# A graph network in one kernel: the ranks of its edge sort counted by partition, and uneven transfers cut in two

## The chip, the cores and the metric

The kernel runs on one core of one Trainium2 chip. A core has five engines that run side by side and wait for each other through semaphores: TensorE (PE) for matrix products, VectorE (DVE), ScalarE (ACT), GpSimd (POOL) and SyncE (SP), which here only issues transfers. Sixteen DMA engines move data between the chip's memory (DRAM) and the on-chip memory, SBUF, of 128 partitions. Products land in PSUM, from which DVE or ACT take them. The metric is the time of one execution on the device, in microseconds (us); lower is better.

## What is computed

Two graph layers on 6250 nodes of 128 features, with 100000 edges (source, destination, weight, 128 edge features), sorted by destination. Each ends in a layer norm over the residual.

```python
# layer 0: two graph convolutions
def gcn_conv(x, src, dst, ew, W, b):
    deg = segment_sum(ew, dst); dinv = where(deg > 0, rsqrt(deg), 0)
    norm = dinv[src] * ew * dinv[dst]
    return segment_sum((x @ W)[src] * norm[:, None], dst) + b
x = layernorm(x + sigmoid(gcn_conv(relu(gcn_conv(x, W1, b1)), W2, b2)))   # with self-loops
# layer 1: attention over edges
z = x @ fc_w.T;  rh = edge_attr @ fc_r_w.T
e = leaky_relu(z[src] @ aw0 + z[dst] @ aw1 + rh @ aw2)
alpha = softmax of e over the edges of one dst
x = layernorm(x + relu(segment_sum(alpha[:, None] * (z[src] + rh), dst) + z @ loop_w))
```

## The kernel before

The edges stand in 49 chunks of 2048 (`CC`), the last of 1696. In a chunk, partition p holds the 16 edges 16p to 16p + 15 (`TC` = 16). As edges are sorted by destination, the destinations of one chunk fall into a window of 144 nodes (`WC`).

Each of the three passes over the edges has to fetch one row of a node table for every edge. Most rows come from a copy of the table in SBUF (`hot`, 48 blocks of 128 nodes as three bf16 parts), picked by products with one-hot masks. For this, the edges of a chunk are once sorted by the source's block: each of the 48 blocks (`BP`) has 32 slots (`CAP`) per chunk. An edge whose rank in its block is 32 or more, or whose source lies in the last block, goes to one of five further groups of 128 slots, whose rows GpSimd fetches from DRAM one by one (`far`, an indirect transfer, L485). Each of these five groups may only reach a fixed part of the window (`far_parts`). If an edge falls outside, or a group overflows, a flag in `odd` starts a slow path at the end.

The sort (`sort`, from L689) runs in batches of up to seven chunks, and beside the first pass. Its generator is stepped by `sort_to` between the pieces of the pass: seven steps that work out the ranks, then seven that place the edges (`ohm`, `ohg`, `put`, the products rec), then one that writes the slots' sources to DRAM (`srd`), from which the pass loads them as a row copied to all partitions (L849) and makes the masks (L853).

A rank step before (L698 to L723): `oh` is the one-hot of each edge's block, 128 x (48 x 16). The rank of an edge is the number of edges of the same block that stand before it, by its place t in the partition and then by partition. That number is summed in PSUM in two halves of 24 blocks (tile r, one buffer of two banks): a product with the strict triangle `trib` counts those of the same t on lower partitions; products with ones count the earlier t, by sums over 2, 4 and 8 places that DVE makes (`a2`, `a4`, `a8`, L703 to L705; the profile calls all three a). ACT copies r to bf16 (`own`, L717), DVE multiplies with `oh` and adds up over the 48 blocks, which leaves one rank for each edge.

In the pass itself (the loop after L860) `pick` makes the products g (L476), ACT scales them (`got`, L481), DVE makes the one-hot of the destinations (`wm`, L491 and L498), ACT weighs the far part of it (L515), and `scatter` sums rows by destination (win, L522). DVE adds the window to the accumulator `acc` (L527). The order of instructions in this stage is the scheduler's; each engine then runs its own list in order.

The second pass has its order written out by hand. Beside it DVE works out the edge scores from the edge features: `load_chunk` loads the next chunk's features (`et`, 16 x 128 numbers on each partition, L994, two buffers), `edge_dots` multiplies and reduces (L980, L981). After the pass the score stage begins, whose first instructions on DVE are a memset of `zero` (L1035) and on SP's queue two stores of it (`adgd`), then loads of source rows (`rk`) and masks.

Where the number of rows is no multiple of 128, a transfer covers what is left: 106 rows of the last node block (L231, L265), 106 partitions of the last chunk (L994), 49 rows of `degr` (L827), and 34, 82 or 114 rows of the softmax (`ad`, L1106).

## Time and profile before

| | |
|---|---|
| time, median of 3 runs | 2352.22 us (2351.19 to 2368.92) |
| the profiled execution | 1995.56 us, of which the span is 1993.8 us |
| mean granted clock of TensorE in it | 0.897 |

The profiled execution is a single one, and shorter than those that were timed. By stages, each row being the busy time in us of PE, PE's weight loads, DVE, ACT and POOL, then the granted clock (1 is full speed), the busy share of the DMA engines, and GB/s:

```profile
0.00:100.00 100.00, 52.41 (x462) 38.92 (x463) 75.07 (x199) 16.95 (x27) 25.95 (x192) 0.98 0.20 50
...
400.00:450.00 50.00, 42.88 (x1105) 38.84 (x1106) 43.79 (x105) 27.51 (x95) 35.48 (x29) 0.97 0.45 130
...
650.00:700.00 50.00, 43.92 (x672) 38.92 (x665) 17.69 (x31) 30.52 (x98) 25.05 (x20) 0.84 0.27 60
...
900.00:1000.00 100.00, 87.81 (x2033) 82.22 (x2033) 93.88 (x106) 69.92 (x225) 83.54 (x55) 0.93 0.75 243
...
1200.00:1300.00 100.00, 50.23 (x873) 40.25 (x874) 73.50 (x199) 22.02 (x53) 16.18 (x12) 0.58 0.50 142
...
1600.00:1700.00 100.00, 87.28 (x1955) 80.73 (x1956) 92.41 (x212) 38.39 (x132) 37.43 (x32) 0.93 0.66 184
```

From 0 to 170 us: loads, degrees, the first table, the first chunks' ranks. To about 640: the first pass with the sort. To 730: the second table. To about 1205: the second pass with the edge scores' dot products. Then the attention stage. In the page's lines and in the timeline, "a<-b" is what an instruction writes and reads, "[3.46 <-ACT own L717]" the time that its engine stood before it and what released it; neighbours of one kind are merged, with their number behind x.

The instructions of a rank step, as groups over 170 to 610 us (busy us in all, mean ns of one, then idle time before them):

```profile
L718 DVE TENSOR_TENSOR own<-own,oh 128x768 bf16<-128x768 bf16 x39 | 21.6, 555 | 21.3 <-ACT own L717 20.9
L698 DVE TENSOR_TENSOR oh<-iota_t,blk 128x768 bf16<-128x768 bf16 x37 | 20.0, 549 | 0.0
...
L703 DVE TENSOR_TENSOR a<-oh 128x384 bf16<-128x384 bf16 x38 | 13.5, 354 | 0.1
L723 DVE TENSOR_REDUCE rank<-own 128x16 f32<-128x96 bf16 x39 | 12.4, 318 | 0.1
...
L704 DVE TENSOR_TENSOR a<-a 128x192 bf16<-128x192 bf16 x38 | 9.6, 254 | 0.6
...
L705 DVE TENSOR_TENSOR a<-a 128x48 bf16<-128x48 bf16 x38 | 7.6, 201 | 0.7
```

These are durations from fetch to end; neighbours on one engine overlap a little, so that the distance from start to start is shorter.

### The profile page before, as it was taken

The page shows a single profiled execution, that of the slowest core. Times are in us where ns is not written, and L with a number is a line of the kernel's source. Part 1 is how long each engine was busy: PE and PEld are TensorE (multiplying, and loading weights), DVE is VectorE, ACT ScalarE, POOL GpSimd, SP SyncE. Part 2 cuts the span into 40 slices and gives each one's busy share as a digit, 9 for nine tenths or more (in the row PEclk, how much of TensorE's full clock was granted, in tenths as well). Part 3 has the DMA queues.
Part 4 walks back from the last instruction along what each step waited for, and adds up shares of the span by engine and source line. Part 5 has one row for each costly group of instructions (what it writes and reads, how often), then busy time and mean ns, then how long its engine had stood idle before and what let it go on. Part 6 is the DMA issues. An engine that isn't in the chain of part 4 may idle for free.

```text
span 1993.8 us, 78720 instructions
## 1 busy us (share of the span) xinstructions
PE 1594.7 (80%) x33767; PEld 1441.7 (72%) x33767; DVE 1633.2 (82%) x3252; ACT 945.4 (47%) x3098; POOL 1105.1 (55%) x953
## 2 busy tenths in 40 slices
PE   2867889989988868789888873568888888988996
PEld 1556878878877757688778762457777778877985
DVE  7788978988976348999989965889989898997764
ACT  1255445455455655667667653123444343435543
POOL 4025666677776548888888861214344353535762
PEclk9978989999998859999989995579999998999998
DMA  2114244244246237777777773646666566655663
GB/s 63 37 44 151 66 117 132 51 139 135 68 123 183 70 123 224 223 237 251 233 226 248 229 235 116 173 106 170 181 162 191 168 183 181 181 163 143 189 171 70
DMA packets 254593, 306.90 MB, mean 154 GB/s; under 512 B 37857, under 2 KB 193255, under 8 KB 247182
## 3 DMA queue, kind: packets, MB, share of 16 engines
q1 hardware_dynamic: 222627, 244.90, 38.9%
q0 software_dynamic: 23520, 48.22, 11.6%
q10 hardware_dynamic: 8088, 8.65, 1.4%
q8 instruction: 268, 4.39, 0.9%
q14 instruction: 90, 0.74, 0.1%
HBM read 260.42 MB, written 41.25 MB: 151 GB/s over the span
## 4 chain that ended last, share of the span: by engine, by line
DVE 38%; PE 37%; DMA 10%; issue 7%; ACT 5%; DVEq 1%; POOL 1%; SPq 0%; ACTq 0%; POOLq 0%
PE win L522 17%; PE g L476 6%; DVE wm L491 6%; DVE et L980 3%; DVE sel L1096 2%; DVE put L764 2%; DVE ohm L759 2%; DMA et<-in_edge_attr_dram 2%; PE rec L1209 2%; PE k L1093 2%; PE mm L333 2%; DMA rk<-srow 2%; ACT got L481 2%; DMA far<-g,sidx 1%; PE r L1239 1%
## 5 line engine op out<-in xcount | busy, mean ns | idle before, releaser
L485 POOL DMA_INDIRECT far<-g,sidx x490 | 729.2, 1488 | 228.4 <-PE win L522 101.1
L481 ACT ACTIVATE got<-g,swt 128x128 f32<-128x128 f32 x1764 | 484.9, 382 | 367.1 <-PE g L476 167.1
L485 POOL DMA_INDIRECT far<-zd,sidx x245 | 310.9, 1269 | 462.4 <-PE win L522 339.5
L522 PE MATMUL win<-wm,got 128*128 128x144 f32 x3528 | 529.1, 308 | 11.6 <-issue 11.5
L522 PEld LDWEIGHTS win<-wm,got 128*128 128x128 f32 x3528 | 492.1, 206 | 29.6 <-issue 20.2
L476 PE MATMUL g<-hot,mask 128*32 128x128 bf16 x21168 | 385.5, 226 | 81.3 <-issue 58.0
L476 PEld LDWEIGHTS <-mask 128*32 128x32 bf16 x21168 | 328.3, 100 | 117.3 <-issue 85.6
L491 DVE TENSOR_TENSOR wm<-iota,sdst 128x1728 f32<-128x1728 f32 x147 | 286.7, 1950 | 3.6 <-DMA g<-rows 3.5
L515 ACT ACTIVATE wm<-wm,swt 128x64 f32<-128x64 f32 (+1 forms) x735 | 201.2, 356 | 83.0 <-DVE wm L498 50.7
L522 PE MATMUL win<-wm,far 128*128 128x64 f32 (+1 forms) x1470 | 189.7, 274 | 19.7 <-DMA far<-g,sidx 15.5
L522 PEld LDWEIGHTS win<-wm,far 128*128 128x128 f32 x1470 | 184.8, 196 | 19.5 <-issue 15.8
L980 DVE TENSOR_TENSOR et<-et,ar_row 128x2048 f32<-128x2048 f32 (+1 forms) x49 | 111.6, 2278 | 25.2 <-DMA et<-in_edge_attr_dram 25.2
L527 DVE TENSOR_TENSOR acc<-acc,win 128x144 f32 x147 | 44.3, 301 | 106.1 <-PE win L522 93.4
L1093 PE MATMUL k<-adp,rk 128*128 128x49 bf16 x2352 | 92.1, 194 | 47.6 <-DVE sel L1096 33.2
L1093 PEld LDWEIGHTS <-rk 128*128 128x128 bf16 x2352 | 84.4, 103 | 59.3 <-issue 30.0
L981 DVE TENSOR_REDUCE dots<-et 128x16 f32<-128x2048 f32 (+1 forms) x49 | 112.0, 2286 | 1.7
L322 POOL TENSOR_TENSOR hot<-low,hot 128x512 bf16<-128x512 f32 x24 | 32.6, 1358 | 140.1 <-DVE hot L321 100.3
L1096 DVE TENSOR_TENSOR sel<-k,ohb 128x392 f32<-128x392 f32 x98 | 83.7, 854 | 4.5 <-PE k L1093 3.9
L764 DVE TENSOR_TENSOR put<-ohg,rec 128x1360 bf16<-128x1360 bf16 x49 | 76.8, 1566 | 0.0
L717 ACT CAST own<-r 128x768 bf16<-128x768 f32 x49 | 39.3, 802 | 70.9 <-PE r L714 50.0
L771 PE MATMUL rec<-put,ohm 128*128 128x90 bf16 x784 | 59.3, 242 | 15.6 <-DVE put L767 14.7
L771 PEld LDWEIGHTS <-ohm 128*128 128x128 bf16 x784 | 55.2, 164 | 21.6 <-DVE put L767 10.8
(397 smaller groups left out, 2317.7 us busy)
## 6 DMA issues: line engine op xcount, KB each, us to landing
et<-in_edge_attr_dram SPq DMA_DIRECT2D x97, 512.0 KB
et<-in_edge_attr_dram SPq DMA_DIRECT2D x48, 1024.0 KB
mask<-masks SPq DMA_DIRECT2D x98, 384.0 KB
rk<-srow SPq DMA_DIRECT2D x98, 256.0 KB
mask<-srd SPq DMA_DIRECT2D x49, 384.0 KB
masks<-mask SPq DMA_DIRECT2D x49, 384.0 KB
far<-g,sidx POOLq DMA_INDIRECT x490
g<-rows SPq DMA_DIRECT2D x24, 256.0 KB
```

Of the source, the lines that this page charges most:

```text
L476: nc.tensor.matmul(ps[32 * q : 32 * q + 32, g, :], mask[:, (g0 + g) * P + 32 * q : (g0 + g) * P + 32 * q + 32], hot[:, 4 * (g0 + g) + q, k ...
L481: nc.scalar.activation(got[:, g, :], ps[:, g, :], AF.Copy, scale=swt[:, c, g0 + g : g0 + g + 1])
L485: nc.gpsimd.indirect_dma_start(out=got, out_offset=None, in_=table[:, :], in_offset=bass.IndirectOffsetOnAxis(ap=sidx[:, c, g : g + 1], ax ...
L491: nc.vector.tensor_tensor(wm[:, : GP * WC].rearrange("p (g w) -> p g w", w=WC), iota[:, None, 1 : WC + 1].to_broadcast([P, GP, WC]), sdst[ ...
L515: nc.scalar.activation(m, m, AF.Copy, scale=swt[:, c, g : g + 1])
L522: nc.tensor.matmul(ps[:, n0 : n0 + m.shape[-1]], rows[g], m, start=g == 0, stop=g == G - 1)
L764: nc.vector.tensor_tensor(put[:, :, : G * F].rearrange("p t (g f) -> p t g f", f=F), ohg[:, :, :, None].to_broadcast([P, TC, G, F]), rec[: ...
L771: nc.tensor.matmul(ps, ohm[:, :, t], put[:, t, :], start=t == 0, stop=t == TC - 1)
L980: nc.vector.tensor_mul(et[:n], et[:n], ar_row[:n, None, :].to_broadcast([n, TC, D]))
L981: nc.vector.tensor_reduce(dots[:n, c, :], et[:n], AX.X, OP.add)
L1093: nc.tensor.matmul(ps[:, s, :], mk[:, s * P : (s + 1) * P], adp[:, 0, k, :NB], start=k == 0, stop=k == 2)
L1096: nc.vector.tensor_mul(sel, ps, ohb.rearrange("p b s -> p s b"))
```

## The change

The rank is counted in another order: by partition first, the partitions taken in a scattered order (partition p at place 79p mod 128), and within a partition by t. `first` is the 128 x 128 table of which partition comes before which, and `lower` the 16 x 16 table of which t comes before which. All edges of earlier partitions are counted by 16 products, one for each t, of `first` with the 48 columns `oh[:, :, t]`, summed in one PSUM tile of 128 x 48 with two buffers. The columns of such a product stand 16 elements (32 bytes) apart. ACT spreads the 48 counts to 48 x 16 as it copies them. Within the partition, DVE compares the 16 blocks with each other (`pairs`), multiplies by `lower` and reduces to 16 numbers (`near`); `near` is added to the ranks once for each batch. The sums a2, a4, a8 and the old products are gone.

Apart from that, a helper `even` cuts a number of rows into the largest multiple of 16 and the rest, and the uneven transfers are issued as two: 106 as 96 and 10, 49 as 48 and 1, 34, 82 and 114 as 32, 80 and 112 and 2.

```diff
@@ constants
+    spread = const.tile([P, P + 1], I32, name="spread")
+    for of, at in ((iota_i[:, :P], slice(0, P)), (iotap_i[:, 0:1], slice(P, P + 1))):
+        nc.vector.tensor_scalar(spread[:, at], of, 79, None, op0=OP.mult)
+        nc.vector.tensor_scalar(spread[:, at], spread[:, at], P - 1, None, op0=OP.bitwise_and)
+    spread_f = const.tile([P, P + 1], F32, name="spread_f")
+    nc.vector.tensor_copy(spread_f, spread)
+    first = const.tile([P, P], BF16, name="first")
+    nc.vector.tensor_scalar(first, spread_f[:, :P], spread_f[:, P:], None, op0=OP.is_gt)
+    lower = const.tile([P, TC, TC], BF16, name="lower")
+    nc.vector.tensor_tensor(lower, iotab[:, None, :TC].to_broadcast([P, TC, TC]),
+                            iotab[:, :TC, None].to_broadcast([P, TC, TC]), op=OP.is_lt)
@@ helper
+    def even(n):
+        cut = n // 16 * 16
+        return [slice(a, b) for a, b in ((0, cut), (cut, n)) if b > a]
@@ store_blocks (load_some, degr, load_chunk, softmax's ad in the same way)
-            eng.dma_start(table[(NB - 1) * P : N, :], of[:tail, NB - 1 - b0, :])
+            for r in even(tail):
+                eng.dma_start(table[(NB - 1) * P + r.start : (NB - 1) * P + r.stop, :], of[r, NB - 1 - b0, :])
@@ load_chunk
-                nc.sync.dma_start(ets[c][:n], ea[c * CC : c * CC + n * TC, :].rearrange("(p t) f -> p t f", t=TC))
+                of = ea[c * CC : c * CC + n * TC, :].rearrange("(p t) f -> p t f", t=TC)
+                for r in even(n):
+                    nc.sync.dma_start(ets[c][r], of[r])
@@ sort
-    ps_r = sorting.enter_context(tc.tile_pool(name="ps_r", bufs=1, space=PSUM))
+    ps_r = sorting.enter_context(tc.tile_pool(name="ps_r", bufs=2, space=PSUM))
...
+            near = sp.tile([P, BATCH, TC], F32, name="near", bufs=1)
...
-                a2 = sp.tile([P, BP, 8], BF16, name="a2")
-                a4 = sp.tile([P, BP, 4], BF16, name="a4")
-                a8 = sp.tile([P, BP, 1], BF16, name="a8")
-                nc.vector.tensor_tensor(a2, oh[:, :, 0:8], oh[:, :, 8:16], op=OP.add)
-                nc.vector.tensor_tensor(a4, a2[:, :, 0:4], a2[:, :, 4:8], op=OP.add)
-                nc.vector.tensor_tensor(a8, a4[:, :, 0:1], a4[:, :, 2:3], op=OP.add)
-                ps = ps_r.tile([P, 2, 512], F32, name="r")
-                for h in range(2):
-                    ks = slice(h * HB, h * HB + HB)
-                    full = ps[:, h, : HB * TC].rearrange("p (k t) -> p k t", t=TC)
-                    nc.tensor.matmul(full, trib, oh[:, ks, :], start=True, stop=False)
-                    nc.tensor.matmul(full[:, :, 8:16], onesb, oh[:, ks, 0:8], start=False, stop=False)
-                    for of, m, w in ((a2, 2, 4), (a4, 4, 2), (a8, 8, 1)):
-                        to = full.rearrange("p k (b i) -> p k b i", b=m)[:, :, :, w : 2 * w]
-                        nc.tensor.matmul(to, onesb, of[:, ks, None, 0:w].to_broadcast([P, HB, m, w]),
-                                         start=False, stop=w == 1)
+                ps = ps_r.tile([P, BP], F32, name="r")
+                for t in range(TC):
+                    nc.tensor.matmul(ps, first, oh[:, :, t], start=t == 0, stop=t == TC - 1)
+                pairs = sp.tile([P, TC, TC], BF16, name="pairs", bufs=1)
+                nc.vector.tensor_tensor(pairs, blk[:, c, :, None].to_broadcast([P, TC, TC]),
+                                        blk[:, c, None, :].to_broadcast([P, TC, TC]), op=OP.is_equal)
+                nc.vector.tensor_mul(pairs, pairs, lower)
+                nc.vector.tensor_reduce(near[:, c - c0, :], pairs, AX.X, OP.add)
                 own = sp.tile([P, BP, TC], BF16, name="own", bufs=2)
-                nc.scalar.copy(own.rearrange("p (h k) t -> p h (k t)", h=2), ps[:, :, : HB * TC])
+                nc.scalar.copy(own, ps[:, :, None].to_broadcast([P, BP, TC]))
                 nc.vector.tensor_mul(own, own, oh)
...
+            nc.vector.tensor_add(r_, r_, near[:, :n])
```

More of the change, by code (lines that the diff above doesn't have):

```diff
@@ L76, in gnn_kernel @@
     BP = 4 * GP
-    HB = BP // 2
     G = GP + GS
@@ L264, in load_some @@
         if b0 + n >= NB:
-            eng.dma_start(to[:tail, NB - 1 - b0, :], of[(NB - 1) * P : N, :])
+            for r in even(tail):
+                eng.dma_start(to[r, NB - 1 - b0, :], of[(NB - 1) * P + r.start : (NB - 1) * P + r.stop, :])
     def transpose_blocks(pool, to, of, first=0, count=NB):
@@ L826, in gnn_kernel @@
             degr = xp.tile([NB, 3, P], F32, name="degr")
-            nc.sync.dma_start(degr, degd.rearrange("k b p -> b k p"))
+            for r in even(NB):
+                nc.sync.dma_start(degr[r], degd.rearrange("k b p -> b k p")[r])
             nc.vector.tensor_add(degr[:, 0, :], degr[:, 0, :], degr[:, 1, :])
@@ L1105, in softmax @@
             ad = lp.tile([P, P], F32, name="ad", bufs=1)
-            nc.sync.dma_start(ad[:R, :], adgd[c0 * CC : c0 * CC + R * P].rearrange("(r j) -> r j", j=P))
+            rows = adgd[c0 * CC : c0 * CC + R * P].rearrange("(r j) -> r j", j=P)
+            for r in even(R):
+                nc.sync.dma_start(ad[r, :], rows[r, :])
             ps = ps_c.tile([P, P], F32, name="rec")
```

## The prediction

> **What bounds the kernel now.** I read the page first, then the busy times of the stage that the change touches (170 to 610 us, the first edge pass, in which the sort runs beside the aggregation), then its chain of waits, its waits, and last the timeline at two places.
>
> ```profile
> span 1993.8 us, 78720 instructions
> PE 1594.7 (80%) x33767; PEld 1441.7 (72%) x33767; DVE 1633.2 (82%) x3252; ACT 945.4 (47%) x3098; POOL 1105.1 (55%) x953
> ```
> ```profile
> 170.00:610.00 440.00, 384.36 (x8477) 352.62 (x8475) 381.23 (x815) 225.86 (x784) 307.49 (x209) 0.93 0.38 109
> ```
> The second fence is one row of the busy times by stretch: PE, PEld, DVE, ACT, POOL, then the granted clock. PE and DVE are each busy 87% of the stage. Neither has room: what one engine gives up is worth something only where the other does not wait already.
>
> ```profile
> by line: PE win L522 17.5%; DVE wm L491 9.8%; DVE put L764 9.5%; DVE ohm L759 8.3%; PE g L476 7.7%; issue 4.6%; DMA mask<-srd 4.5%; PE r L714 4.0%; PE rec L771 3.1%; ACT own L717 2.9%; ACT got L481 2.6%; DVE ohg L761 2.5%; PE r L710 2.4%; D
> ```
> ```profile
> PE rec L738 <- DVE tot L736: 22.8, 6, 5.9
> ...
> DVE own L718 <- ACT own L717: 20.9, 13, 2.9
> ...
> PE r L710 <- ACT own L717: 13.9, 6, 3.5
> ```
> First the chain of waits of that stretch, then its waits (us, times, longest). Adding up the chain's pieces, the rank products r (L710, L711, L714) hold 31.5 us of these 440, the sums a2, a4, a8 that feed them (L703 to L705) 10.8, the eviction `own` 12.7. The edited code is thus about 10% of this stage's path, not more.
>
> ```profile
> 253.61 0.35 ACT L515 ACTIVATE wm<-wm,swt 128x64 f32<-128x64 f32 x1 [2.30 <-DVE wm L498]
> 253.86 0.78 ACT L717 CAST own<-r 128x768 bf16<-128x768 f32 x1
> 254.69 0.48 PE L710 MATMUL r<-oh,trib 128*128 128x384 bf16 x1 [3.46 <-ACT own L717]
> 255.77 0.52 PE L710 MATMUL r<-oh,trib 128*128 128x384 bf16 x1
> ```
> Here PE stands 3.46 us because r has one buffer: the eviction is queued on ACT behind a weighting that waits for DVE. Afterwards the same 384-column product takes 0.48 us, against 0.33 before: the clock has been halved.
>
> ```profile
> 1192.88 0.58 PE L522 MATMUL win<-wm,far 128*128 128x16 f32 x2 [1.37 <-DMA far<-g,sidx]
> 1200.69 2.29 DVE L980 TENSOR_TENSOR et<-et,ar_row 106x2048 f32<-106x2048 f32 x1 [22.03 <-DMA et<-in_edge_attr_dram]
> ...
> 1206.42 0.17 DVE L1035 MEMSET zero<- 1x128 f32 x1 [0.36 <-issue]
> ```
> ```profile
> 1166.04 34.63 DMA et<-in_edge_attr_dram
> 1207.59 5.28 DMA mask<-masks
> ```
> At the end of the second pass the chain is one transfer: the last chunk's 106 rows of edge attributes take 34.6 us, and DVE stands 22.03 us for them. The first such load, of 128 rows, was issued at 733.65 and used at 738.88.
>
> **The change part by part.** *Products.* Per chunk go two halves of one 384-column and four 192-column products. From start to start these take 0.16, 0.08 and 3 x 0.08 to 0.11 us, 0.57 a half, 1.13 a chunk. In come 16 products of 48 columns, each reading every sixteenth element of `oh`. Two rows bound their price:
>
> ```profile
> 1391.14 0.77 PE L1093 MATMUL k<-adp,rk 128*128 128x49 bf16 x24
> 1402.32 1.12 PE L1209 MATMUL rec<-put,ohm 128*128 128x51 bf16 x16 [1.00 <-DVE put L1205]
> ```
> L1093 has the width and contiguous operands: (0.77 - 0.18)/23 = 26 ns a product. L1209 has the width, 16 products summed in one tile, and one operand (the weights) at that same step of 16: (1.12 - 0.2)/15 = 61 to 62 ns. The step costs 36 ns there. I take 62 ns, 0.99 us a chunk; low end 26 ns (0.42 us), high end 128 ns (2.05 us), as a moving operand at a step is in no row. On the chain: 31.5 x (0.99/1.13 - 1) = -3.9 us (ends -20 and +25).
>
> Two rules of the Trainium skill speak against this part. "TensorE: Matmul & The Clock Gate", Back-to-back issue gap, gives a stream of weight load and product at 128 columns about 81 ns a product; 16 would cost 1.30 us, and this part +4.7 us on the chain. L1093's 26 ns with a weight load before each product shows that the floor lies lower here, so I keep 62. "SBUF — State Buffer", Door 1: The DMA port swizzle, says in a note that accesses which enter a new 16-byte line each time pay a penalty; a step of 32 bytes does. L1209 agrees for the weights; if a single moving stream pays more than the weights do, the price goes to the high end. That is my slower rival.
>
> *DVE.* Out: a2, a4, a8, from start to start 0.27, 0.17, 0.12 = 0.56 us. In: a compare of 256 (ohg, 272 elements, starts at 0.35 us intervals), a product of 256 bf16 (own's sums: 384 in 0.27, 192 in 0.17, so 0.21) and a reduction of 256 to 16 (that of 96 takes 0.23 to the next start, 160 more elements at about 1 ns: 0.33 to 0.40) = 0.89 us or a little more; and one add of about 0.2 us per batch. Net +0.33 us a chunk, 14 us over the 42 chunks of the stretch. Of the a's 23.5 us of work, 10.8 (46%) lay on the chain. Taking that share for the new 37.4 us: 17.2 - 10.8 = +6.4 us (ends: -10.8 if all of it hides, +14).
>
> *Waits.* The products now need `oh` alone, and r has two buffers in the same two banks. The stop at 254.69 goes: its detour over ACT (0.35 + 0.70 us on the chain), the r products at half clock (2.33 against 1.13) and the 111 g products at half clock (3.18 against about 1.7): 3.7 us. There are six such waits, not all as long, and DVE is next: between 243 and 281 us it is busy 31.5 of 38 us and gets 7 x 0.33 = 2.3 more. I count 60%: -13 us (ends 0 and -22). The wait for `tot` (22.8 us) stays, with some of the new compares now queued ahead of it on DVE.
>
> *The last edge load.* 96 rows and 10 rows. Before, by its packets, two 8 KB rows were in flight at a time; by "DMA: Bandwidth & Descriptors", Why a DMA increments its semaphore, 96 rows spread over 16 engines and 10 over 10. I expect it at about 1172 us, ahead of DVE's need at 1178.7. Next late: the last far rows, which release PE's last product at 1192.88. The second add to acc stands behind it, then the memset of `zero` (1206.42), then on SP's queue, in this order, the two adgd stores, an rk load and the mask load of 1207.59 on which PE waits. So the memset moves to 1192.9 + 0.6 + 0.5 = 1194, 12.4 us earlier; with less traffic on two engines the far rows land a little sooner: -13.5 us (ends -4 and -21; `hot` loads 1152 KB at a time beside it whatever happens).
>
> *Other splits.* Each costs about 0.25 us of SP's queue (ad's eight, x1d, zd, xt, fin, out, g twice, degr) and ACT's once (xs). Covers: for ad, DVE waited 0.5 us in all; degr is used at 107.52 while DVE never stops; the tail of x1, the g stores and the last fin load (3.0 us on the chain at 1977) trade an issue against a shorter transfer: 0, between -3 and +3. *Constants:* nine DVE rows, about 1.5 us, beside the input loads that hold the chain from 1.88 to 10.39 us: nothing, at most 1.5. *First seven chunks:* DVE holds most of the chain from 98 to 170 us, so 7 x 0.33: +2 us.
>
> Sum: -3.9 + 6.4 - 13 - 13.5 + 2 = -22 us on 1995.56 us (1993.8 of span and 1.8 around it), -1.1%. The runs shown have a median of 2352.22 us, 357 us above the profiled one, and no view says where those are. I carry the share over: -26, **2326 us**.
>
> **The rivals.**
> *PE is slower in the timed runs.* If the 357 us are PE at half clock, PE bounds the stage. At half clock the r products cost 2.33 us a chunk, 16 products perhaps 1.18 (74 ns, as L771's bursts stretch from 1.19 to 1.4 us). With half of the stage so: -0.6 x 49 = -29 us, the DVE work hides, waits and load as above: -53, about 2298. For: the profile's clock falls to 0.5 after each stop. Against: DVE is as full as PE in it.
> *It is given back.* DVE, with 14 us more, takes the room that the waits leave, and the far rows and `hot` loads hold the next stage anyway: -5 us, about 2347, no change. For: 31.5 of 38 us busy.
> *Slower: the step of 32 bytes.* If one moving column at a step costs 2.7 ns (128 ns a product), PE gets 16 x 66 ns x 42 = 44 us more than I count, all on its path: -22 + 44 = +22, about 2378. It decides from 22/(16 x 42) + 62 = 95 ns a product, 2 ns a column.
> *Not what it says.* Other edges overflow now, and a window missed would start the slow path. Counted from the input in both orders, at most 534 of a chunk overflow (640 fit) and none leaves its window; I give this nothing.
>
> **How the numbers follow.** Forecast 0.42, PE-bound 0.28, given back 0.13, slower 0.17. About 1% (2329 us) is what a measurement here can tell from no change. My own case straddles it: 0.25 beyond, 0.17 within; PE-bound is all beyond; given back within; of the slower one 0.13 beyond and 0.04 within. Faster 0.53, same 0.34, slower 0.13. The range, 2280 to 2376, runs from below the PE-bound case to the slower one; what is left out is a saving at 26 ns with everything else at its good end, and a price above 128 ns.
>
> **What would show it.** Starts of the 16 products 62 ns apart (26 or over 95 decide between the cases); no wait of PE's r for `own`; pairs, its product and near at 0.35, 0.21 and 0.33 to 0.40 us between starts; DVE above 90% busy in the first pass; no idle time before the last `et`, and the memset of `zero` 12 to 14 us sooner after the last far rows' issue. Wrong if the first pass is longer than before, or if the mask load after the second pass comes as late as now.

## The result, and the profile after

| | median | ratio to before, 95% interval |
|---|---|---|
| before | 2357.51 us (2327.11 to 2373.34, 20 runs) | |
| after | 2375.2 us (2353.02 to 2386.21, 20 runs) | 1.0100 (1.0075 to 1.0126) |

The ratios leave out executions more than 1.5% above the fastest of their kernel; medians and ranges are of all.

The change made the kernel 1.0% slower, where I had forecast 1.1% faster. The profiled execution of the changed kernel has 2362.94 us, as long as its timed runs. From its page, the span and the busy time of each engine:

```profile
span 2361.1 us, 79341 instructions
PE 1821.7 (77%) x34061; PEld 1587.0 (67%) x34061; DVE 1651.7 (70%) x3267; ACT 953.3 (40%) x3098; POOL 1080.2 (46%) x953
```

Against the page of before, 367 us have been added to the span, but only 294 products and 15 DVE instructions. Most of the added time can't be the change's. The kernel before, profiled once more, confirms it: 2401.24 us. From the waits of the profile shown before the prediction (us in all, times, longest us), and then of the new profile of the same kernel:

```profile
PEld L476 <- issue: 85.6, 69, 7.1
...
PE g L476 <- issue: 58.0, 42, 5.0
```
```profile
PEld L476 <- issue: 407.9, 692, 10.3
PE g L476 <- issue: 269.8, 558, 2.2
```

"Issue" means that the engine waited for nothing that the profile shows. The nearest reading is that PE had no instruction to run; no view shows this directly. (The two rows overlap, as weight loads run beside products.) The timeline shows what this looks like, first in the profile shown before the prediction, then in the new one:

```profile
302.12 0.91 PE L476 MATMUL g<-hot,mask 128*32 128x128 bf16 x52
```
```profile
337.16 0.26 PE L476 MATMUL g<-hot,mask 128*32 128x128 bf16 x4 [0.50 <-issue]
337.90 0.29 PE L476 MATMUL g<-hot,mask 128*32 128x128 bf16 x5 [0.48 <-issue]
338.65 0.28 PE L476 MATMUL g<-hot,mask 128*32 128x128 bf16 x4 [0.46 <-issue]
```

Undisturbed, 52 of the short g products take 0.91 us. In the new profile a handful comes every 0.74 us, for some microseconds at a time. Counted over the trace, 603 neighbouring g products start more than 0.3 us apart, 419 us in all, against 42 with 66 us in the first profile. The difference, 353 us, is most of the 405 us between the two spans. The changed kernel's profile has 559 such gaps with 374 us: the change neither makes nor cures them.

So this kernel has two levels, about 1990 us and about 2355 to 2400 us; the runs that were made together, one kernel after another on one chip, lay at one of them. The profile of before had been taken at the first level, the times at the second. The level isn't tied to the numbered chip: number 12 had 1988.53 us for the kernel before at one time and 2353.66 us later. I call them the 1990 level and the 2355 level; where an expectation below says "on a chip where the kernel before takes 1990 us", the level is meant.

The stage of the ranks is compared from 170 us to 785 us at the 2355 level and to 650 us at the 1990 level. The rank products from 170 us on all lie in these stretches, but the first pass itself ends some 40 to 55 us later, with the 49th addition to `acc`: at 679.2 us in the profile shown before the prediction, not at the 640 us of its list of stages. Here is the stage as one row of the busy times by stretch (PE, PEld, DVE, ACT, POOL, then the granted clock): first the changed kernel at the 2355 level, then at the 1990 level (the run after_again below).

```profile
170.00:785.00 615.00, 492.35 (x9249) 435.77 (x9248) 409.61 (x851) 244.50 (x842) 309.38 (x227) 0.81 0.30 89
```
```profile
170.00:650.00 480.00, 422.79 (x9259) 402.77 (x9257) 408.58 (x851) 240.98 (x838) 316.38 (x225) 0.91 0.39 115
```

DVE has the same work in both, 409 us, which is 67% of the stage at the 2355 level and 85% at the other. PE is at 80% at the 2355 level and 88% at the other; a large part of what is missing there is the gaps just shown. The chain of waits says who is left on the path; here its shares by line over the same stretches, of the kernel before at the 2355 level, the changed one there, and the changed one at the 1990 level:

```profile
by line: PE win L522 28.1%; PE g L476 24.6%; issue 17.1%; PE rec L771 7.7%; PE r L714 4.4%; PE r L710 2.2%; DMA mask<-srd 2.0%; DVE wm L491 1.8%; another core or an unknown queue 1.6%; ACT own L717 1.4%; DVE own L722 1.1%; DVE own L718 1.1%
```
```profile
by line: PE win L542 28.9%; PE g L496 24.1%; issue 16.6%; PE r L722 9.2%; PE rec L785 6.4%; DVE put L778 3.1%; DVE ohm L773 2.5%; DVE wm L511 2.4%; DMA mask<-srd 1.9%; DVE ohg L775 0.5%; another core or an unknown queue 0.5%; DVE wm L518 0.
```
```profile
by line: PE win L542 23.5%; PE g L496 11.1%; PE r L722 9.6%; DVE put L778 8.3%; DVE ohm L773 7.9%; DVE wm L511 7.4%; issue 6.4%; PE rec L785 5.3%; DMA mask<-srd 3.4%; DVE ohg L775 2.4%; ACT got L501 1.5%; DVE wm L518 1.5%; DVE put L781 1.3%
```

At the 2355 level the rank products of the kernel before hold 46 us (4.4% and 2.2% of 615 us, and 5.7 us of L711, which stands below the end of its row), those of the changed kernel 57 us (9.2%). At the 1990 level they hold 9.6% of 480 us, 46 us, where the prediction read 31.5 us in the kernel before. The products have become some 10 us more of the path at the one level and 15 us at the other, where I had forecast 3.9 us less. The group of these products, on the page of the changed kernel, and one burst of its timeline:

```profile
L722 PE MATMUL r<-oh,first 128*128 128x48 bf16 x784 | 78.8, 268 | 9.8 <-DVE oh L718 8.4 <-issue 0.8
```
```profile
402.52 1.58 PE L722 MATMUL r<-oh,first 128*128 128x48 bf16 x16
```

The wait for `own` is gone from the group, as forecast. But a burst of 16 takes 1.58 us: from start to start the median is 89 ns, 1.42 us a chunk, where I had 62 ns. It is 89 ns both where the granted clock is 0.5 and where it is 1.

### The profile page after: what moved, and what is told of

Same layout as the page of the kernel before. It is cut to its first block, busy times and chain, and to the rows that moved or that the text cites. A ratio compares the mean times of both kernels' runs of the same rounds, so it can differ in the third digit from the quotient of the medians.

```text
span 2361.1 us, 79341 instructions
## 1 busy us (share of the span) xinstructions
PE 1821.7 (77%) x34061; PEld 1587.0 (67%) x34061; DVE 1651.7 (70%) x3267; ACT 953.3 (40%) x3098; POOL 1080.2 (46%) x953
## 4 chain that ended last, share of the span: by engine, by line
PE 61%; DVE 15%; issue 12%; another core or an unknown queue 4%; ACT 3%; DMA 2%; POOL 1%; ACTq 0%; SPq 0%; DVEq 0%; POOLq 0%
PE win L542 24%; PE g L496 18%; PE r L722 3%; PE rec L1228 2%; PE k L1110 2%; PE r L1258 2%; DVE wm L511 2%; DVE sel L1113 2%; PE rec L785 2%; PE mm L353 2%; PE rec L1269 2%; ACT got L501 1%; DVE put L778 1%; DVE ohm L773 1%
## 5 line engine op out<-in xcount | busy, mean ns | idle before, releaser
L505 POOL DMA_INDIRECT far<-g,sidx x490 | 713.1, 1455 | 461.6 <-PE win L542 326.9
L496 PE MATMUL g<-hot,mask 128*32 128x128 bf16 x21168 | 563.8, 246 | 264.8 <-issue 241.4
L496 PEld LDWEIGHTS <-mask 128*32 128x32 bf16 x21168 | 415.1, 109 | 383.2 <-issue 363.2
L542 PE MATMUL win<-wm,got 128*128 128x144 f32 x3528 | 547.3, 314 | 7.3 <-issue 6.0
L542 PEld LDWEIGHTS win<-wm,got 128*128 128x128 f32 x3528 | 508.2, 212 | 32.7 <-issue 24.3
L1110 PE MATMUL k<-adp,rk 128*128 128x49 bf16 x2352 | 104.9, 199 | 61.4 <-DVE sel L1113 36.4
L773 DVE TENSOR_TENSOR ohm<-iota_t,pm 128x2048 bf16<-128x2048 bf16 x49 | 59.7, 1218 | 49.0 <-PE rec L785 27.1
L731 DVE TENSOR_TENSOR own<-own,oh 128x768 bf16<-128x768 bf16 x49 | 28.1, 573 | 91.7 <-ACT own L730 89.6
L722 PE MATMUL r<-oh,first 128*128 128x48 bf16 x784 | 78.8, 268 | 9.8 <-DVE oh L718 8.4
L722 PEld LDWEIGHTS <-first 128*128 128x128 bf16 x784 | 68.7, 120 | 16.0 <-issue 8.2
```

Of the source, the lines that this page charges most:

```text
L496: nc.tensor.matmul(ps[32 * q : 32 * q + 32, g, :], mask[:, (g0 + g) * P + 32 * q : (g0 + g) * P + 32 * q + 32], hot[:, 4 * (g0 + g) + q, k ...
L505: nc.gpsimd.indirect_dma_start(out=got, out_offset=None, in_=table[:, :], in_offset=bass.IndirectOffsetOnAxis(ap=sidx[:, c, g : g + 1], ax ...
L542: nc.tensor.matmul(ps[:, n0 : n0 + m.shape[-1]], rows[g], m, start=g == 0, stop=g == G - 1)
L722: nc.tensor.matmul(ps, first, oh[:, :, t], start=t == 0, stop=t == TC - 1)
L773: nc.vector.tensor_tensor(ohm, iota_t, pm[:, c, None, :].to_broadcast([P, P, TC]), op=OP.is_equal)
L1110: nc.tensor.matmul(ps[:, s, :], mk[:, s * P : (s + 1) * P], adp[:, 0, k, :NB], start=k == 0, stop=k == 2)
```

## The experiments

Four theories, which the expectations call by letter. A: PE is held by its supply of instructions, and what counts is how many a chunk has, 32 for 20. B: what counts is the time of the products that read at a step of 32 bytes. C: DVE's new work counts. D: the cut transfers cost.

**The kernel before once more** (no edit).

> The kernel before, unchanged, profiled once more. The profile shown of it has 1995.56 us; its timed runs have a median near 2355 us, and the profile of the changed kernel (2362.94 us) agrees with that kernel's timed runs. Theory 'the profile was of a faster stretch of the chip': a new profile has about 2330 to 2370 us, a granted clock near 0.84 in place of 0.897, and the idle time of PE put down to its own instruction issue rises from 86 + 58 us (weight loads and products of the g group) to some hundreds, as in the changed kernel (363 + 241 us). Rival 'the new waits come from the change': it has less than 200 us of such idle time whatever its time.

2401.24 us, clock 0.838, 408 and 270 us of issue: the rival falls, as shown above.

**One part at a time.** The ranks alone are the changed kernel with

```diff
     def even(n):
-        cut = n // 16 * 16
-        return [slice(a, b) for a, b in ((0, cut), (cut, n)) if b > a]
+        return [slice(0, n)]
```

> The new ranks alone, every transfer whole as before. Theory A (PE is short of instructions in the timed runs, and the change gives it 32 a chunk for 20): all of the loss is here, 10 to 30 us slower than before, and the profile's PE idle time on its own issue is as large as in the changed kernel. Theory B (each strided product costs 89 ns, so that PE has 1.42 us for 1.13 us a chunk at full clock): 49 x 0.29 = 14 us slower at most, about 0 to 14. Theory C (DVE has 0.33 us more a chunk): 16 us slower at most, and DVE over 85% busy in the first pass. Theory D (the loss is from the cut transfers): same as before within 0.3%.

1.0052 (1.0024 to 1.0081) of the kernel before, 2412.79 us for 2398.88.

> The new ranks alone, transfers whole. Measured: 1.0052 where the kernel before takes 2399 us. Where it takes about 1990 us the whole change has 0.9947 and the cut transfers alone 0.9917; if the parts add up the ranks have 1.0030 there, 6 us slower, with the first pass 8 to 12 us longer than before and all else alike. Rival 'each part needs the other': below 1.000 or above 1.006 there.

At the 1990 level 1.0042 (1.0022 to 1.0063). The first pass ends at 693.2 us in this profile, by the start of the 49th addition to `acc`, for 679.2 us in the one shown of before.

The cut transfers alone are the kernel before with `even` and the five places that use it, without `first`, `lower`, `pairs` and `near`.

> The cut transfers alone, ranks as before. Theory D: 20 us or more slower. Theories A to C: not slower; if the wait for the last edge load (25 us of DVE in the profile of before) is on the path in the timed runs, 10 to 20 us faster, 0.4 to 0.9%; if its cover is the far rows' memset and mask in any case, within 0.3%.

1.0002 (0.9972 to 1.0032) at the 2355 level. A gain of the size that I had forecast (13.5 us, 0.6%) is excluded there. By this ratio D falls, but the medians of all runs stand further apart, 2412.65 us for 2398.88 (0.6%), so a cost of that size is not excluded at this level.

> The cut transfers alone. Measured: 1.0002 (0.9972 to 1.0032) on a chip where the kernel before takes 2399 us. On a chip where it takes about 1990 us the last edge load was on the path (25 us of DVE waiting in the profile shown, 1.7 to 3.5 us in the changed kernel's): theory 'the cut transfers gain there, and the ranks lose 10 us in the first pass' has 0.990 to 0.994 on such a chip, 12 to 20 us faster; on one where it takes about 2390 us, 0.998 to 1.002 again. Rival 'the gain comes from the ranks' has 0.998 to 1.002 on both.

0.9917 (0.9894 to 0.9940) at the 1990 level, 16 us faster. The changed kernel itself, at that level:

> The changed kernel once more, on the chip of the three kernels beside it, as their zero. Measured so far: 1.0100 of the kernel before (1.0075 to 1.0126) for it, 1.0052 (1.0024 to 1.0081) for its ranks alone on another chip, 1.0002 for its cut transfers alone. If the two parts add up, 1.0025 to 1.0100; 'the cut transfers cost only together with the ranks' needs 1.0075 or more again.

0.9947 (0.9925 to 0.9969), 1980.34 us for 1990.32. There the change is faster, by half of what I forecast. The parts add up: 0.42% slower and 0.83% faster make 0.41% faster, 0.53% was measured. At the 2355 level they make 0.54% slower, and 1.00% was measured at another time; the intervals are too wide to say that the parts don't add up there. (By the medians of all runs they are 0.58% and 0.57%, and the whole 0.75%.)

What the cut load of the last edges does is seen at the end of the second pass, at the last far rows (`far`), the use of the load (`et`) and the memset of `zero`. The timeline of the ranks alone at the 1990 level (load whole), then of the changed kernel at that level (load cut), then of the kernel before at the 2355 level (load whole):

```profile
1195.91 0.94 POOL L504 DMA_INDIRECT far<-g,sidx  x1 [0.30 <-issue]
...
1216.03 2.29 DVE L994 TENSOR_TENSOR et<-et,ar_row 106x2048 f32<-106x2048 f32 x1 [23.06 <-DMA et<-in_edge_attr_dram]
1221.77 0.17 DVE L1051 MEMSET zero<- 1x128 f32 x1 [0.36 <-issue]
```
```profile
1196.59 2.28 DVE L995 TENSOR_TENSOR et<-et,ar_row 106x2048 f32<-106x2048 f32 x1
1199.99 0.94 POOL L505 DMA_INDIRECT far<-g,sidx  x1 [0.30 <-issue]
1210.08 0.17 DVE L1052 MEMSET zero<- 1x128 f32 x1 [0.34 <-DMA zd<-zrows]
```
```profile
1426.69 0.94 POOL L485 DMA_INDIRECT far<-g,sidx  x1 [0.30 <-issue]
1432.21 2.29 DVE L980 TENSOR_TENSOR et<-et,ar_row 106x2048 f32<-106x2048 f32 x1 [5.96 <-DMA et<-in_edge_attr_dram]
1437.94 0.17 DVE L1035 MEMSET zero<- 1x128 f32 x1 [0.36 <-DMA hot<-hz]
```

Whole, the load keeps DVE waiting 23.06 us at the 1990 level, and the memset of `zero` comes 25.9 us after the last far rows were issued (23.6 us in the profile shown of before). Cut, DVE doesn't wait, and it comes 10.1 us after: 13.5 to 16 us sooner. The packets agree with the reason that the prediction gave: of the 8 KB rows of the whole load at most four are in flight at once, and the last one ends 35 us after the issue (ranks alone at the 1990 level); cut, up to 18 are, and the last one ends after 8.4 us. At the 2355 level the whole load is nearly hidden in this profile: the wait is 5.96 us, and the memset comes 11.2 us after the last far rows, against 9.7 us with the cut load in the changed kernel's first profile. There 1.5 us are left to win. (The profile of the ranks alone at that level has 19.8 us, with a wait of 15.8; how well the load is covered differs from run to run.)

**More of one cost.** Each of these adds to the changed kernel; what it adds leaves the ranks as they are. The first three write to unused columns of r's bank, ahead of the 16 products that count:

```diff
-                ps = ps_r.tile([P, BP], F32, name="r")
+                both = ps_r.tile([P, 2, BP], F32, name="r")
+                for t in range(TC):
+                    nc.tensor.matmul(both[:, 1, :], first, oh[:, :, t], start=t == 0, stop=t == TC - 1)
+                ps = both[:, 0, :]
```

with `oh[:, :, t]` (48 columns at the step of 32 bytes), `oh[:, 3 * t : 3 * t + 3, :]` (48 adjacent columns), or one column. The fourth makes `pairs`, its product and `near` twice.

> The changed kernel with 16 more products of 48 columns at the step of 32 bytes in each chunk, written to unused columns of the same bank: 32 more instructions and 16 x 89 ns = 1.42 us more of PE a chunk. Theory A (the number of instructions on PE counts, 20 ns each, from 12.5 us for 12 x 49 in the ranks alone): 32 x 49 x 20 ns = 31 us, 1.013 of the changed kernel, and the same as with the thin products. Theory B (the time of the strided read counts): 70 us, 1.029, and far from the thin products. Theory C (DVE's 0.33 us a chunk is the loss; PE has room in this stage): within 0.3% of the changed kernel.

> The changed kernel with 16 more products of one column in each chunk: 32 more instructions, next to no columns. Theory A: 31 us, 1.013 of the changed kernel. Theory B: 16 x about 25 ns x 49 = 20 us at most, and under half of what the strided products add. Theory C: within 0.3% of the changed kernel.

> The changed kernel with DVE's compare of 16 by 16, its product and its sum made twice in each chunk, the second time over the first: some 0.9 us of DVE a chunk, 44 us in all, nothing on PE. Theory C (DVE bounds the sort's stage): 30 to 44 us, 1.013 to 1.019 of the changed kernel. Theories A and B (PE bounds it, DVE has a quarter of its time free): within 0.4%, under 10 us.

> 16 more strided products of 48 columns a chunk than the changed kernel. Measured on a chip where the kernel before takes 1990 us: 64 us more than the changed kernel (2044 for 1980). Where it takes about 2390 us: theory A (there PE is held by its instruction supply, and each instruction costs about 20 ns whatever it does): 31 us more than the changed kernel, ratio to before 1.018 to 1.023. Theory B (the strided read costs its 89 ns there too): 60 to 70 us more, ratio 1.031 to 1.039.

> 16 more products of one column a chunk than the changed kernel. Measured on a chip where the kernel before takes 1990 us: 14 us more (1994 for 1980), 9 ns an instruction. Where it takes about 2390 us: theory A: 31 us more, the same as for the strided products, ratio to before 1.018 to 1.023. Theory B: 14 us again, ratio 1.011 to 1.016, and far below that of the strided products.

> The changed kernel with 16 more products of 48 adjacent columns in each chunk (the same size as the strided ones, other columns). Measured where the kernel before takes 1990 us: 16 strided ones cost 64 us, 16 of one column 14 us. Theory B (what costs is the step of 32 bytes, not the columns): near the thin products, 14 to 24 us more than the changed kernel, ratio 1.002 to 1.007 there. Rival 'the 48 columns cost, not their step': 55 to 65 us more, 1.022 to 1.028. Where the kernel before takes about 2390 us, theory A has the strided, the adjacent and the thin products alike.

All of these ran at the 1990 level, where the changed kernel has 0.9947:

| 16 more products a chunk, or DVE's part twice | ratio to before | over the changed kernel |
|---|---|---|
| 48 columns at a step of 32 bytes | 1.0255 (1.0210 to 1.0301), 1.0263 (1.0218 to 1.0307) | 61 to 63 us |
| 48 adjacent columns | 1.0044 (1.0024 to 1.0065) | 19 us |
| one column | 1.0007 (0.9990 to 1.0024), 1.0036 (1.0018 to 1.0053) | 12 to 18 us |
| compare, product and sum on DVE | 1.0071 (1.0038 to 1.0104) | 25 us |

(The last column is the difference of the ratios times 1990 us, each uncertain by 6 to 10 us.) 48 adjacent columns cost about as little as one column; the same number at the step costs three times as much. It is neither the number of instructions nor of columns, but the step: A falls at this level, B holds. The timeline of the kernel with 16 adjacent products (L722) ahead of the 16 strided ones (L725) shows both side by side:

```profile
330.87 0.57 PE L722 MATMUL r<-oh,first 128*128 128x48 bf16 x16
331.28 1.59 PE L725 MATMUL r<-oh,first 128*128 128x48 bf16 x16
```

DVE's 0.87 us a chunk (42 us) cost 25 us: its work counts at this level too, at some 60%.

> 16 more strided products a chunk than the changed kernel, once more. Where the kernel before takes 1990 us: 1.026 as twice before. Where it takes about 2390 us: theory A (each instruction costs about 20 ns there) 1.013 of the changed kernel, 1.018 to 1.023 of the kernel before; theory B (the strided read costs its 89 ns there too) 1.029 of the changed kernel, 1.031 to 1.039 of the kernel before.

At the 2355 level 1.0198 (1.0138 to 1.0258): the number that A gave. Against the 1.0100 of the changed kernel, from another chip, that is 23 us for 70 us of PE; against 1.0054, the sum of its parts, 34 us. Strided products beyond those of the change cost less there; why is not shown. This alone speaks for A; the next experiment speaks against it.

**The step taken away.** The planes are laid out one after another, so that the same 16 products read adjacent columns; ACT and DVE follow in that order.

```diff
-                oh = sp.tile([P, BP, TC], BF16, name="oh")
-                nc.vector.tensor_tensor(oh, iota_t[:, :BP, :], blk[:, c, None, :].to_broadcast([P, BP, TC]),
-                                        op=OP.is_equal)
+                oh = sp.tile([P, TC, BP], BF16, name="oh")
+                nc.vector.tensor_tensor(oh, iotab[:, None, :BP].to_broadcast([P, TC, BP]),
+                                        blk[:, c, :, None].to_broadcast([P, TC, BP]), op=OP.is_equal)
...
-                    nc.tensor.matmul(ps, first, oh[:, :, t], start=t == 0, stop=t == TC - 1)
+                    nc.tensor.matmul(ps, first, oh[:, t, :], start=t == 0, stop=t == TC - 1)
...
```

> The changed kernel with the planes laid out one after another (oh and own as 16 by 48 in place of 48 by 16), so that each product reads 48 adjacent columns: 16 products of the same size, without the step of 32 bytes. On PE 16 x (89 - 30) ns = 0.9 us a chunk less, 46 us in all. DVE's compare that makes oh takes its two operands in another order and is longer: by the compare for ohg (431 ns for 272 elements) 1.0 to 1.2 us for 0.55, 22 to 32 us more in all. Theory B (the step is what made PE's part of the change cost): by the prices measured (64 us for 70 of PE, 28 us for 44 of DVE) 42 less and 14 to 20 more, 22 to 28 us faster than the changed kernel: 0.981 to 0.984 where the kernel before takes 1990 us. Theory C, as the single product showed it (PE's time is only worth something while DVE keeps up): within 10 us of the changed kernel or slower, 0.990 to 1.005 there. Where the kernel before takes about 2390 us, theory A (each instruction on PE costs the same whatever it reads) has no gain: DVE's 22 to 32 us may hide or not, 1.002 to 1.012.

0.9936 (0.9908 to 0.9964) at the 2355 level. Once more:

> Planes of 48 adjacent columns once more. Measured: 0.9936 where the kernel before takes 2352 us, with 26 to 30 ns from one product's start to the next for 89, and 949 ns for DVE's compare for 549. Where it takes about 1990 us: by the prices measured there, 16 x 0.06 us x 49 = 47 us of PE less at 0.9 (42) and 0.4 us x 49 = 20 us of DVE less its sum's gain of 8, at 0.64 (8 more): 34 us faster than the changed kernel, 0.978. If these prices don't add up there (the single product came out 18 us slower than the changed kernel, by the ratios, where they said 32 us faster), DVE bounds the stage on such a chip, and it is 0.990 to 1.003.

The 2355 level again: 0.9881 (0.9829 to 0.9933). With the same number of products, 1.6 to 2.2% less than the changed kernel's 1.0100, 39 to 52 us (28 to 41 us if its parts' 1.0054 is taken): A, as an explanation of the change, falls at this level as well. The chain of waits over this kernel's first pass (170 to 745 us), and two bursts of its timeline in the stage:

```profile
by line: PE win L542 25.7%; PE g L496 22.8%; issue 14.4%; PE rec L785 7.3%; DMA mask<-srd 4.3%; another core or an unknown queue 3.9%; PE r L722 3.3%; DVE wm L511 2.6%; DVE ohm L773 2.4%; DVE put L778 2.1%; ACT got L501 1.5%; DMA srd<-srT 1
```
```profile
254.42 0.97 PE L722 MATMUL r<-oh,first 128*128 128x48 bf16 x32
271.02 1.46 PE L722 MATMUL r<-oh,first 128*128 128x48 bf16 x32
```

The rank products fall from 57 us of the path to 19 (3.3% of 575 us), about as much as the gain. A product takes (0.97 - 0.18)/31 = 25 ns from start to start, or 41 ns in the second burst. The granted clock is 1 in the first and 0.5 in the second: these do follow the clock. DVE pays for it: its compare for `oh` takes 949 ns for 549. At the 1990 level, where DVE is on the path, this version was not measured.

**Fewer products.** DVE adds the 16 planes up by halves, and one product counts:

```diff
+                few, w = oh, TC
+                while w > 1:
+                    w //= 2
+                    half = sp.tile([P, BP, w], BF16, name=f"a{w}")
+                    nc.vector.tensor_tensor(half, few[:, :, 0:w], few[:, :, w : 2 * w], op=OP.add)
+                    few = half
-                for t in range(TC):
-                    nc.tensor.matmul(ps, first, oh[:, :, t], start=t == 0, stop=t == TC - 1)
+                for t in range(w):
+                    nc.tensor.matmul(ps, first, few[:, :, t], start=t == 0, stop=t == w - 1)
```

> The changed kernel with its 16 planes added up by DVE in four steps (halves of 8, 4, 2 and 1 planes), and one product of 48 adjacent columns a chunk in place of 16: 2 instructions on PE a chunk for 32 (1470 fewer in all), and some 0.7 us more of DVE. Theory A (instructions on PE): 1470 instructions at up to 73 ns in the starved stretches, so 25 to 100 us faster than the changed kernel, ratio to before 0.965 to 0.995. Theory B (the strided read): 1.3 us less PE a chunk, at most 65 us faster than the changed kernel, same range if PE bounds the stage. Theory C (DVE bounds the stage): 0.7 x 49 = 34 us slower than the changed kernel, ratio to before 1.02 or more.

0.9939 (0.9915 to 0.9963) at the 2355 level, where DVE has room.

> The changed kernel with 16 planes added up by DVE and one product of 48 adjacent columns a chunk. Measured: 0.9939 where the kernel before takes 2399 us. From the runs on the chip with 1990 us: 16 strided products cost 64 us (1.3 us a chunk) and 0.9 us of DVE a chunk 28 us. If these prices add up: 15 strided products fewer are 60 us less, three to four adds of DVE (about 0.9 us) 28 us more: 32 us faster than the changed kernel on such a chip, ratio 0.979. Theory C (DVE bounds the stage as soon as PE has less): 0.995 or more there.

1.0050 (1.0025 to 1.0074) at the 1990 level, 20 us slower than the changed kernel where the added prices said 32 us faster. The row of its first pass, and two of its waits there:

```profile
170.00:650.00 480.00, 378.39 (x8562) 352.92 (x8565) 435.96 (x1019) 240.23 (x833) 297.57 (x225) 0.89 0.38 112
```
```profile
PE r L728 <- DVE a L725: 25.1, 17, 3.7
PEld L496 <- DVE mask L874: 19.5, 9, 3.3
```

PE has fallen to 79%, DVE risen to 91%, and PE now waits for DVE, for the sums and for the masks. The prices of single additions don't hold for it: DVE now counts more than PE, which is C, once PE has less.

**Less work on DVE.** `pairs`, its product and `near` for four chunks in one instruction each, ahead of the loop over the chunks:

```diff
+            pairs = sp.tile([P, 4, TC, TC], BF16, name="pairs", bufs=1)
+            for a in range(0, n, 4):
+                m = min(4, n - a)
+                at = slice(c0 + a, c0 + a + m)
+                nc.vector.tensor_tensor(pairs[:, :m], blk[:, at, :, None].to_broadcast([P, m, TC, TC]),
+                                        blk[:, at, None, :].to_broadcast([P, m, TC, TC]), op=OP.is_equal)
+                nc.vector.tensor_mul(pairs[:, :m], pairs[:, :m], lower[:, None].to_broadcast([P, m, TC, TC]))
+                nc.vector.tensor_reduce(near[:, a : a + m, :], pairs[:, :m], AX.X, OP.add)
...
```

> The changed kernel with the compare of 16 by 16, its product and its sum made for four chunks in one instruction each, ahead of the chunks' loop, in place of once a chunk: 42 DVE instructions for 147, the same elements. A chunk's three take about 1.1 us now; by their 256 elements at about 1 ns an element for compare and sum, 0.4 ns for the product, the rest, some 0.3 to 0.4 us a chunk, is their start-up: 15 to 20 us of DVE less. By the price measured for DVE in this stage (28 us for 44) 10 to 12 us faster than the changed kernel: ratio 0.989 where the kernel before takes 1990 us. Theories A and B (PE alone bounds the stage): within 0.3% of the changed kernel, 0.992 to 0.998 there, 1.002 to 1.010 where it takes about 2390 us.

0.9998 (0.9973 to 1.0023) at the 1990 level: the expectation was missed, it is 10 us slower than the changed kernel instead of 10 to 12 us faster, though DVE's busy time in 172 to 650 us fell from 407 to 397 us. Of its waits in the first pass:

```profile
PE r L730 <- DVE oh L726: 18.9, 6, 3.2
```

Six times, once a batch, PE stands some 3 us for `oh`, which now stands behind two blocks of DVE work; in the changed kernel this wait is 2.1 us in all. Cheaper work in the wrong place turned into a wait.

## Why the prediction was wrong

**The time of the runs.** I made the sum on a profile 357 us shorter than the timed runs, noted that "no view says where those are", and carried the share over. This step failed. Most of the 357 us are gaps before PE's g products for which the profile shows no wait. With them DVE nearly leaves the path (50 us of the chain between 170 and 785 us in the kernel before, for 205 us between 170 and 640 us in the first profile), PE's waits for `own` shrink, and the cut load gains nothing, whereas a strided product still takes its 89 ns. At the level of the profile the direction was right, 0.53% faster where I had 1.1%, in part by luck (the third pass, below).

**Products: the term that was mis-sized.** I had two rows of the same width, 26 ns with adjacent operands and 62 ns with the weights at a step of 32 bytes, and took 62. Measured are 89 ns, 1.85 ns a column. On the chain this part is +15 us at the 1990 level and +10 us at the 2355 level, instead of -3.9. The term decides the sign at the 2355 level: with adjacent columns, and all else of the change, the kernel came out faster than before there (0.9936 and 0.9881). The row was the nearest one, but its step was on the other operand. The rival "Slower: the step of 32 bytes" named the mechanism; its 128 ns were too many, and its point of decision (95 ns) was reckoned with gains that aren't there at the 2355 level. That its 2378 us lies so near the measured 2375.2 is luck: too high a price stood against gains that did not come. The rule of the Trainium skill in "SBUF — State Buffer", Door 1: The DMA port swizzle, that each access to a new line of 16 bytes pays a penalty, was weighed there and agrees in kind: adjacent columns 26 ns a product, the step 89. No run here tried a step between 2 and 32 bytes, so where the penalty begins isn't shown. The other rule that the prediction weighed is for 128 columns and has no bearing on 48: adjacent ones took 25 to 26 ns.

**DVE.** Its parts came as forecast: from start to start 0.34, 0.20 and 0.33 us in, 0.28, 0.17 and 0.12 out, +0.30 us a chunk for my +0.33. The stretch holds 39 chunks, not 42; ten, not seven, come before 170 us, which moves 1 us between two terms. The share on the chain was too high: `pairs`, its product and `near` hold 5.0 us of it at the 1990 level, where I took 17.2. "Above 90% busy" did not come: 85% at the 1990 level.

**Waits.** PE no longer waits for ACT's `own`, in any profile of the new ranks. What that is worth is not shown: the end of the first pass came 14 and 11 us later in the two profiles at the 1990 level (ranks alone, whole change), and the pieces of the chain, which shift from one engine to another, don't add up to it. At the 2355 level there was little to win, as the kernel before had lost only 4.1 us in such waits between 170 and 785 us, for 13.9 between 170 and 610 in the first profile.

**The last edge load.** -13.5 us was right at the 1990 level: 13.5 to 16 us by the memset, 16 us by the times of the cut transfers alone. At the 2355 level nothing of it is seen in the times (1.0002). The other splits at nothing agree with both ratios.

**The rivals.** "PE is slower in the timed runs" was right about its first half, wrong about the cause (not a lower clock alone, granted 0.84 for 0.90, but 353 us of gaps before products) and about the price. "It is given back" finds no support at the 2355 level: what was to be given back was not gained there.

**What stays open.** Why PE's g products come slowly at the 2355 level. The Trainium skill ("Runtime: NRT & Kernel Launch", Instruction fetch mechanics) has each engine's instructions fetched in blocks by a queue of its own, mostly hidden. That queue's row of the page (packets, MB, share of 16 engines' span), in the profile shown of before and in its repeat at the 2355 level, doesn't show the cause:

```profile
q8 instruction: 268, 4.39, 0.9%
```
```profile
q8 instruction: 268, 4.39, 0.8%
```

The same 268 packets of 16 KB took no longer in all (0.9% of 1994 us, 0.8% of 2399). Nor do the gaps follow the fetches: in the repeat a gap begins, in the median, 4.5 us after the last packet of that queue and 4.0 us before the next. Open is also why the whole change measured 24 us at the 2355 level (18 us by its medians) while the products' 10 us on the chain and the ranks alone (12.5 us) account for some two fifths to two thirds; if the cut transfers cost what the medians of all their runs say (14 us), nothing is missing. The changed kernel and its parts were not measured side by side there.

The forecast has no term for the third pass, and there lies a part of what was measured at the 1990 level. From its first addition to `acc` to its last it takes, in the profile shown of before and in the changed kernel at that level:

```profile
1302.40:1974.40 672.00, 576.94 (x13185) 535.05 (x13185) 577.48 (x1336) 272.92 (x948) 298.27 (x232) 0.94 0.61 166
```
```profile
1307.00:1960.20 653.20, 559.34 (x13166) 518.48 (x13162) 575.02 (x1333) 271.98 (x948) 297.62 (x234) 0.96 0.63 171
```

That is 18.8 us less, in single profiles, though no rank is worked out there any more. It is 663.9 us with the cut transfers alone, 658.5 with the ranks alone, and 666.4 in the version with one product. So the ranks' 14 us in the first pass and their 8 us (1.0042) in the whole time differ by a stage that the change hardly touches; why it is shorter is not known.

No version was best at both levels: the cut transfers alone at 1990 us (0.9917), the adjacent planes at 2355 us (0.9936 and 0.9881, with the single product's 0.9939 level with the first of these), untried at the other.

## What to carry to other kernels

Before a sum is made on a profile, ask whether the profile and the timed runs are at the same level; where they are far apart (357 us here), forecast for each and find out which engine is bound in each. A price read from a neighbouring row is good for the operand whose layout it has: the step of 32 bytes made a product 89 ns in the moving operand and 62 ns in the weights. A layout with adjacent columns can be worth more than fewer products. Where two engines are both near full, a price measured by adding work to one need not hold when work is moved to the other: 32 us faster was reckoned for the single product, 20 us slower measured.

## What the runs showed of the hardware

- A product whose 48 moving columns stand 32 bytes apart takes 89 ns from start to start, at a granted clock of 0.5 and of 1 alike; with adjacent columns it takes 25 ns at 1 and 41 ns at 0.5. With weights at the same step (L1209) it was 61 to 62 ns.
- PE can stand between short products without any wait that the profile shows: three to five products every 0.74 us for some microseconds, and 353 us more of such gaps in one profile of a program than in another. In the changed kernel's profile with such gaps, a burst of strided products kept its 89 ns (402.52 us above).
- A load of 106 rows of 8 KB (35.66 us in the ranks alone at the 1990 level, by the chain of waits) no longer holds DVE once it is issued as 96 and 10 (8.4 us by its packets, in the changed kernel at that level).
